# Additions on GpSimd turned into adding transfers in a macaron block with a state-space layer

## The chip, the cores and the metric

The kernel runs on one core of a Trainium2 chip. The metric is the device time of one launch in microseconds (us); the kernel before took 755.14 us, the median of three runs (752.95 to 756.56). A core has five engines with a queue of instructions each: TensorE (PE in the profile), VectorE (DVE), ScalarE (ACT), GpSimd (POOL) and SyncE (SP), which here only begins transfers. Each engine works through its queue in order. An instruction that waits for a semaphore holds up everything behind it on its engine. Transfers (DMAs) are carried by 16 DMA engines that all queues share. A transfer's issue takes time on the engine that begins it, and the transfer lands later.

## The reference

The input is x, 4096 tokens (two sequences of 2048) of 256 numbers, all in 32-bit floating point. Cut to what matters:

```python
def ffn(x):                                  # 8 groups of 512 tokens, each with weights of its own
    h1 = einsum('gmh,goh->gmo', x.reshape(8, 512, 256), W1) + b1[:, None, :]
    return (einsum('gmo,gho->gmh', h1, W2) + b2[:, None, :]).reshape(x.shape)

def ssm(x):
    x_in, z = split(x @ Wi.T + bi)           # 512 channels each
    u  = silu(causal_conv(x_in, conv_w) + conv_b)        # 4 taps for each channel
    dt = softplus(x_in[..., :32] @ Wdt.T + bdt)
    for t in tokens:                         # 512 channels x 16 states
        h = h * exp(dt_t * A) + dt_t * Bm * u_t
        y_t = (h * Cm).sum(-1)
    return (y * silu(z)) @ Wo.T + bo + x * Dv.mean()

x = x + 0.5 * ffn(layernorm(x))
x = x + ssm(layernorm(x))
x = x + 0.5 * ffn(layernorm(x))
```

The network between the two products of `ffn` has no nonlinearity, so the kernel multiplies W1 and W2 once for each group.

## The kernel before, in words

The tokens are taken in four batches of 1024 (`s` from 0 to 3; two batches make a sequence), each in two halves of 512 (`h`). The 512 channels of the state-space layer are taken in four quarters of 128 (`q`). A quarter of a batch is laid out as two tiles of 128 partitions by 512 (`u` = 0 and 1): 64 channels by two halves of the tokens. The first and the last quarter of the whole run are laid out otherwise ("wide": 128 channels, 512 tokens).

The backbone is a row of 256 positions, 64 for each batch and 16 for each quarter. At each position VectorE runs one scan (L698) of 128 by 1024, which takes a decay tile `dec` (ScalarE's exponential, L685, issued three positions ahead) and a drive `pv` in PSUM, which TensorE spreads over the states from the drive `v` (L669). TensorE then reduces the scan's output `g` with the weights `wy` (L707). Everything else is fitted in beside it: the table `PL` gives each step of the preparation a place relative to a position, and the program emits the steps position by position. So the order within each engine's queue is fixed by hand, and no scheduler moves it.

For each quarter the class `Prepare` makes the drive in the 16 positions before it is used. TensorE makes the projections (`inner_pe`), ScalarE writes them into `xi` with the last three columns of the tokens before in front (`inner_act`, `edges`), and `centre` (L531) starts the convolution in the tile `u`, with the tap that needs no shift and the bias. Then come six calls of `tap`: taps 2, 1 and 0 for both tiles, at places t0 to t5 of the table, most of them one or two positions apart. Each call is two GpSimd instructions: a product of shifted `xi` and the channel's weight into the tile `tap` (L536), and the addition of `tap` to `u` (L537). Then `silu` (L604) runs on ScalarE over the whole of `u`. It needs another table of functions, so a table load stands before it; the two Silus of `z` (L601) follow, and a table load back. GpSimd multiplies u by dt into `v` (`drive`, L637), and TensorE spreads that (`spread_v`, L669). The second quarter of the first batch has an order of its own: its taps run three in a row for each tile (places z0 to z2, y0 to y2), and each tile has a Tanh (L582) in place of Silu. The first quarter takes its taps on VectorE.

The tokens themselves lie in tiles `x` of 128 by 4 by 256. Twice a network's result and once the layer's result are added to such a tile. On GpSimd `bias` (L402) adds the network's combined bias row `bc` to all tokens of a tile, `residual` (L454) scales them, `residual_bias` (L458) adds `bo`, and the results of TensorE are added in halves at L421 and L748. VectorE takes the statistics of the layernorm from the tile once the second of its halves is there (`stats_of`, L329); GpSimd then finds the factors (`newton`, L353 to L360) and normalises (L370).

Buffers come from pools with a fixed number of tiles for each name; an instruction that writes a reused tile waits until the last reader of the old contents is done. The tile `tap` has one buffer (pool `p1`), also used for `tz` (L590) and, at the start, for `par_g` (L207). The combined weights `wc` have five (pool `p6`), one for each of the eight groups in turn. Weights, tokens and the copies of `dt` into `rep` (L653) are transfers that SP begins.

Of the kernel before, what the change touches and what calls it, by code (L numbers as in the profile page):

```python
# [28 lines left out]
F32 = mybir.dt.float32  # L29
AF = mybir.ActivationFunctionType  # L30
ALU = mybir.AluOpType
AX = mybir.AxisListType

P = 128
DM = 256
# [9 lines left out]
GT = 4  # L45
NQ = DI // P
# [3 lines left out]
NM = 4  # L50
NH = DM // P
NO = INTER // P
CH = 512
# [21 lines left out]
def macaron_kernel(ctx: ExitStack, tc: tile.TileContext, x, wi_t, wo_t, wdt_t, par, w1, w2_t, b1, b2, bo, out):  # L75
    nc = tc.nc
    V, S, T, GP = nc.vector, nc.scalar, nc.tensor, nc.gpsimd
# [2 lines left out]
    wpool = ctx.enter_context(tc.tile_pool(name="wpool", bufs=2))  # L80
    p1 = ctx.enter_context(tc.tile_pool(name="p1", bufs=1))
    p2 = ctx.enter_context(tc.tile_pool(name="p2", bufs=2))
    p6 = ctx.enter_context(tc.tile_pool(name="p6", bufs=5))
    p3 = ctx.enter_context(tc.tile_pool(name="p3", bufs=3))
    p4 = ctx.enter_context(tc.tile_pool(name="p4", bufs=4))
    p5 = ctx.enter_context(tc.tile_pool(name="p5", bufs=5))
# [6 lines left out]
    def softplus(o, i, bias):  # L93
        return S.activation(o, i, AF.Softplus, bias=bias)
# [38 lines left out]
    bo_all = const.tile([P, 1, DM], F32, name="bo_all")  # L133
# [70 lines left out]
    sel32 = early[:, NPAIR * 2 * NM :][:, :32]  # L204
    sel_rep = const.tile([P, 2, P], F32, name="sel_rep")
    GP.memset(sel_rep, 0.0)
    par_g = p1.tile([P, 3, NQ, 4, NM], F32, tag="tap", name="par_g")  # L207
    a_log, b_g, c_g = (par_g[:, t].rearrange("p q b m -> p (q b m)") for t in range(3))
    neg_a = const.tile([P, NPAIR * 2 * NM], F32, name="neg_a")
    cb_g = early[:, : NPAIR * 2 * NM].rearrange("p (a b) -> p a b", b=1)  # L210
# [41 lines left out]
    wc, bc, held_row, held_wc = {}, {}, {}, {}  # L252
# [132 lines left out]
    class Ffn(Norm):  # L385
# [13 lines left out]
            return self.xt[pair]  # L399

        def bias(self, eng):
            eng.tensor_tensor(self.xs, self.xs, bc[self.g].to_broadcast((P, GT, DM)), ALU.add)  # L402

        def product(self, pair, bias=False):
            pt = self.pt[pair] = bank(f"pf_{self.name}_{pair}")
            for k in range(2):
                o = pt[:, k * DM : (k + 1) * DM]
                for hh in range(NH):
                    T.matmul(o, lhsT=self.xt[pair][:, hh, k * P : (k + 1) * P], rhs=wc[self.g][:, hh, :],  # L409
                             start=(hh == 0), stop=(hh == NH - 1 and not bias))  # L410
                if bias:
                    spread_row(o, held_row[self.g], False)
# [16 lines left out]
    class Second(Norm):  # L429
# [25 lines left out]
                                 ALU.mult, ALU.add)  # L455

        def residual_bias(self):
            GP.tensor_tensor(self.xs, self.xs, bo_all.to_broadcast((P, GT, DM)), ALU.add)  # L458

# [7 lines left out]
    class Prepare:  # L469
# [62 lines left out]
                         scale=self.par(C_CW, NK, u, NK - 1))  # L532

        def tap(self, k, u):
            tap = p1.tile([P, CH], F32, tag="tap", name=f"tap_{self.n}_{k}_{u}")
            GP.tensor_scalar(tap, self.xi[:, u, k : k + CH], self.par(C_CW, NK, u, k), 0.0, ALU.mult, ALU.add)  # L536
            GP.tensor_tensor(self.u[:, u, :], self.u[:, u, :], tap, ALU.add)  # L537

        def tap_dve(self, k, u):
            V.scalar_tensor_tensor(self.u[:, u, :], self.xi[:, u, k : k + CH], self.par(C_CW, NK, u, k),  # L540
# [46 lines left out]
        def gate_z(self, u):  # L587

            z = zs[self.s, self.q]
            self.tz = p1.tile([P, CH], F32, tag="tap", name="tz")  # L590
            S.activation(z[:, u, :], self.pt["z", u], AF.Identity, bias=self.par(C_BI + NQ, 1, u))
            S.activation(self.tz, z[:, u, :], AF.Tanh, scale=0.5)
            self.pt.pop(("z", u))
# [79 lines left out]
    def place_of(t):  # L673
        s, j = divmod(t // NPOS, NPAIR)
        return s, j, *ORDER[t % NPOS]
# [233 lines left out]
    f = second[1]  # L909
# [112 lines left out]
    for t in range(end):  # L1022
        s, j, k, m = place_of(t)
# [76 lines left out]
```

## Time and profile before

| What | Value |
|---|---|
| median of three runs | 755.14 us |
| the profiled execution | 757.39 us |
| its span, first to last instruction | 755.6 us |
| PE, DVE, ACT, POOL busy | 640.1, 639.0, 527.7, 513.7 us |
| POOL on the chain that ended last | 24% of the span |
| granted clock of TensorE, mean | 0.934 |
| DMA: bytes moved, share of the 16 engines on SP's queue | 62.29 MB, 29.4% |

The busy shares are means over stages with different limits. The chain follows the work that ended last back from the end, at each step to what released it. A line of a group gives the source line, the engine, the operation, output and inputs, their shapes and the count; then the busy time in us and the mean of one in ns; then the idle time of the engine just before, and what ended most of it. A line of the waits names who waited for whom, the us in all, the number of times and the longest. A line of the DMA issues gives the line of the tiles, the queue, the count, the size of one and the median us from issue to landing; the issuing time itself is not counted as busy. A line of the timeline has the start and the duration in us.

### The profile page before, as it was taken

The page shows a single profiled execution, that of the slowest core. Times are in us where ns is not written, and L with a number is a line of the kernel's source. Part 1 is how long each engine was busy: PE and PEld are TensorE (multiplying, and loading weights), DVE is VectorE, ACT ScalarE, POOL GpSimd, SP SyncE. Part 2 cuts the span into 40 slices and gives each one's busy share as a digit, 9 for nine tenths or more (in the row PEclk, how much of TensorE's full clock was granted, in tenths as well). Part 3 has the DMA queues.
Part 4 walks back from the last instruction along what each step waited for, and adds up shares of the span by engine and source line. Part 5 has one row for each costly group of instructions (what it writes and reads, how often), then busy time and mean ns, then how long its engine had stood idle before and what let it go on. Part 6 is the DMA issues. An engine that isn't in the chain of part 4 may idle for free.

```text
span 755.6 us, 10374 instructions
## 1 busy us (share of the span) xinstructions
PE 640.1 (85%) x3422; PEld 274.3 (36%) x3422; DVE 639.0 (85%) x553; ACT 527.7 (70%) x658; POOL 513.7 (68%) x821
## 2 busy tenths in 40 slices
PE   9998797994778999897886999897697989777866
PEld 6634241540212554442221654442121434212444
DVE  3487589794899989877899998867898999999994
ACT  3467786682799667756799677656799777868631
POOL 6125658999854878989853797989964778753421
PEclk9999697996899999999799999999799999897979
DMA  8274224152122326334122226313122222322101
GB/s 295 79 218 118 56 85 126 38 152 49 28 57 57 77 63 162 109 103 130 28 57 57 70 64 159 100 56 82 32 57 56 57 56 58 112 56 56 29 1 56
DMA packets 42789, 62.29 MB, mean 82 GB/s; under 512 B 12536, under 2 KB 22128, under 8 KB 42736
## 3 DMA queue, kind: packets, MB, share of 16 engines
q1 hardware_dynamic: 41344, 59.84, 29.4%
q0 software_dynamic: 720, 1.24, 0.6%
q8 instruction: 27, 0.44, 0.3%
q10 hardware_dynamic: 672, 0.56, 0.2%
q14 instruction: 26, 0.21, 0.1%
HBM read 24.08 MB, written 4.19 MB: 37 GB/s over the span
## 4 chain that ended last, share of the span: by engine, by line
PE 36%; POOL 24%; DVE 16%; ACT 10%; issue 8%; DMA 4%; SPq 2%; ACTq 0%; DVEq 0%; POOLq 0%
DVE g L698 13%; POOL u L537 6%; PE po L739 6%; PE pwc L266 6%; PE py L707 6%; ACT dec L685 5%; PE pv L669 4%; POOL tap L536 3%; POOL x L421 3%; PE pf_f L409 3%; PE pxi L495 2%; PE pz L495 2%; POOL x L402 2%; SPq L653 2%; DMA x<-in_x 2%
## 5 line engine op out<-in xcount | busy, mean ns | idle before, releaser
L685 ACT ACTIVATE dec<-rep,neg_a 128x1024 f32<-128x1024 f32 (+1 forms) x280 | 286.0, 1058 | 78.0 <-DVE g L698 69.4
L698 DVE TENSOR_TENSOR_SCAN g<-dec,state,pv 128x1024 f32<-128x1024 f32 (+1 forms) x160 | 309.3, 2002 | 22.3 <-PE py L707 8.3
L698 DVE TENSOR_TENSOR_SCAN g<-dec,pv 128x1024 f32<-128x1024 f32 (+1 forms) x128 | 265.2, 2132 | 23.5 <-PE pv L669 8.6
L707 PE MATMUL py<-g,wy 128*32 128x512 f32 x1024 | 161.5, 652 | 39.7 <-ACT ev_y L714 22.1
L537 POOL TENSOR_TENSOR u<-u,tap 128x512 f32<-128x512 f32 x90 | 114.2, 1269 | 10.9 <-ACT u L531 3.4
L669 PE MATMUL pv<-v,sel_rep 64*128 64x512 f32 (+1 forms) x256 | 77.6, 702 | 27.1 <-POOL v L637 11.7
L700 POOL COPY state<-g 128x1 f32<-128x1 f32 x160 | 27.7, 186 | 81.2 <-DVE g L698 81.2
L718 POOL TENSOR_TENSOR z<-ev_y,z 128x512 f32<-128x512 f32 x31 | 39.5, 1275 | 50.7 <-ACT ev_y L714 50.7
L409 PE MATMUL pf_f<-wc,xnt_f 128*128 128x256 f32 x256 | 66.1, 401 | 7.2 <-ACT xnt_f L380 4.8
L707 PEld LDWEIGHTS py<-g,wy 128*32 128x32 f32 x1024 | 24.0, 112 | 132.3 <-issue 65.3
L536 POOL TENSOR_SCALAR tap<-xi,par_p 128x512 f32<-128x512 f32 x84 | 58.1, 692 | 9.6 <-DMA xi<-xi 6.1
L266 PE MATMUL pwc<-w,w 128*128 128x256 f32 x256 | 61.8, 388 | 0.6 <-DMA w<-in_w_t 0.3
L495 PE MATMUL pz<-xn2t,wi_sb 128*64 128x512 f32 x224 | 60.3, 665 | 1.3 <-ACT ev_f L417 1.3
L409 PEld LDWEIGHTS pf_f<-wc,xnt_f 128*128 128x128 f32 x256 | 47.6, 196 | 30.5 <-ACT xnt_f L380 9.6
L266 PEld LDWEIGHTS pwc<-w,w 128*128 128x128 f32 x256 | 46.6, 190 | 21.1 <-issue 11.1
L739 PE MATMUL po<-wo_sb,z 64*128 64x256 f32 x448 | 52.8, 386 | 1.6 <-POOL z L718 1.6
L495 PE MATMUL pxi<-xn2t,wi_sb 128*64 128x512 f32 x224 | 51.1, 598 | 0.0
L402 POOL TENSOR_TENSOR x<-x,bc 128x1024 f32<-128x1024 f32 x14 | 33.1, 2362 | 24.3 <-ACT xn_f L368 24.2
L739 PEld LDWEIGHTS po<-wo_sb,z 64*128 64x128 f32 x448 | 42.7, 189 | 16.1 <-issue 7.9
L669 PEld LDWEIGHTS pv<-v,sel_rep 64*128 64x128 f32 (+1 forms) x256 | 20.5, 198 | 74.2 <-DVE g L698 31.2
L637 POOL TENSOR_TENSOR v<-u,dt 128x512 f32<-128x512 f32 x28 | 35.0, 1270 | 6.9 <-ACT u L604 6.9
L380 ACT COPY xnt_f<-ptr_f 128x512 f32<-128x512 f32 x31 | 18.0, 588 | 27.2 <-PE ptr_f L377 22.9
(158 smaller groups left out, 759.3 us busy)
## 6 DMA issues: line engine op xcount, KB each, us to landing
rep<-dt SPq DMA_DIRECT2D x496, 64.0 KB, 2.0
w<-in_w SPq DMA_DIRECT2D x16, 512.0 KB, 4.9
w<-in_w_t SPq DMA_DIRECT2D x16, 512.0 KB, 6.5
x<-in_x SPq DMA_DIRECT2D x7, 512.0 KB, 5.6
out<-x SPq DMA_DIRECT2D x6, 512.0 KB, 3.0
wi_sb<-in_wi_t SPq DMA_DIRECT2D x1, 1024.0 KB, 13.7
wo_sb<-in_wo_t SPq DMA_DIRECT2D x2, 512.0 KB, 6.6
out<-x SPq DMA_DIRECT2D x4, 256.0 KB, 2.2
```

Of the source, the lines that this page charges most:

```text
L266: T.matmul(pt, lhsT=a[:, oc, hh * P : (hh + 1) * P], rhs=b[:, oc, :], start=(k == 0 and oc == 0), stop=(k == 1 and oc == NO // 2 - 1),)
L402: eng.tensor_tensor(self.xs, self.xs, bc[self.g].to_broadcast((P, GT, DM)), ALU.add)
L409: T.matmul(o, lhsT=self.xt[pair][:, hh, k * P : (k + 1) * P], rhs=wc[self.g][:, hh, :], start=(hh == 0), stop=(hh == NH - 1 and not bias))
L495: T.matmul(pt[h * HC : (h + 1) * HC, :], lhsT=wi_sb[:, hh, k : k + HC], rhs=xn2t[self.s, h][:, hh, :], start=(hh == 0), stop=(hh == NH - 1))
L536: GP.tensor_scalar(tap, self.xi[:, u, k : k + CH], self.par(C_CW, NK, u, k), 0.0, ALU.mult, ALU.add)
L537: GP.tensor_tensor(self.u[:, u, :], self.u[:, u, :], tap, ALU.add)
L669: T.matmul(t[:, c * CH : (c + 1) * CH], lhsT=sel_rep[r, c if is_wide(s, j) else a, :], rhs=v_sb[s, j // NJ2][r, j % NJ2, :], start=True, s ...
L685: S.activation(decs[t][:, c * w : (c + 1) * w], part, AF.Exp, scale=neg_a[:, i : i + 1])
L698: V.tensor_tensor_scan(g[:, r], dec[:, r], v[:, r], 0.0 if first else state[:, i : i + 1], ALU.mult, ALU.add)
L707: T.matmul(pys[s, j][rows(is_wide(s, j), a, c), :], lhsT=wy[:, column(s, j, a, c, m), :], rhs=gs[a, m][:, c * CH : (c + 1) * CH], start=(m ...
L718: GP.tensor_tensor(z, held_ev.pop((s, j)), z, ALU.mult)
L739: T.matmul(held_po[s, pair][h][:, k * DM : (k + 1) * DM], lhsT=lhsT, rhs=rhs, start=((q, i) == parts[0]), stop=((q, i) == parts[-1]))
```

## The change

Three additions on GpSimd become transfers that GpSimd begins and that add to their destination: the tap's addition to `u`, and the addition of `bc` and of `bo` to a tile of tokens. A bias row is read four times by the transfer, once for each group of 256 numbers of a partition. `tap` moves to the pool with two buffers, and with it the other two tiles of that name. The pool of `wc` has four buffers, not five. The program places the waits: a reader of `u` or of `x` waits for the landing, the next addition to the same tile waits for the landing of the one before, and the product that reuses a tap buffer waits for the landing of the transfer that reads it.

```diff
-    p6 = ctx.enter_context(tc.tile_pool(name="p6", bufs=5))
+    p6 = ctx.enter_context(tc.tile_pool(name="p6", bufs=4))
...
-    par_g = p1.tile([P, 3, NQ, 4, NM], F32, tag="tap", name="par_g")
+    par_g = p2.tile([P, 3, NQ, 4, NM], F32, tag="tap", name="par_g")
...
         def bias(self, eng):
-            eng.tensor_tensor(self.xs, self.xs, bc[self.g].to_broadcast((P, GT, DM)), ALU.add)
+            GP.dma_start(self.xs, bc[self.g].to_broadcast((P, GT, DM)), accum_op=ALU.add)
...
         def residual_bias(self):
-            GP.tensor_tensor(self.xs, self.xs, bo_all.to_broadcast((P, GT, DM)), ALU.add)
+            GP.dma_start(self.xs, bo_all.to_broadcast((P, GT, DM)), accum_op=ALU.add)
...
         def tap(self, k, u):
-            tap = p1.tile([P, CH], F32, tag="tap", name=f"tap_{self.n}_{k}_{u}")
+            tap = p2.tile([P, CH], F32, tag="tap", name=f"tap_{self.n}_{k}_{u}")
             GP.tensor_scalar(tap, self.xi[:, u, k : k + CH], self.par(C_CW, NK, u, k), 0.0, ALU.mult, ALU.add)
-            GP.tensor_tensor(self.u[:, u, :], self.u[:, u, :], tap, ALU.add)
+            GP.dma_start(self.u[:, u, :], tap, accum_op=ALU.add)
...
         def gate_z(self, u):
-            self.tz = p1.tile([P, CH], F32, tag="tap", name="tz")
+            self.tz = p2.tile([P, CH], F32, tag="tap", name="tz")
```

## The prediction

> **What bounds the kernel now.** I read the page first (busy shares, then the chain that ended last), then the waits, then the timeline round the places where the change acts, then the DMA issues.
>
> ```profile
> PE 36%; POOL 24%; DVE 16%; ACT 10%; issue 8%; DMA 4%; SPq 2%; ACTq 0%; DVEq 0%; POOLq 0%
> ...
> L537 POOL TENSOR_TENSOR u<-u,tap 128x512 f32<-128x512 f32 x90 | 114.2, 1269 | 10.9 <-ACT u L531 3.4
> L402 POOL TENSOR_TENSOR x<-x,bc 128x1024 f32<-128x1024 f32 x14 | 33.1, 2362 | 24.3 <-ACT xn_f L368 24.2
> ```
>
> No engine is full (PE and DVE 85%, ACT 70%, POOL 68%). The chain changes hands: POOL carries it in a few stretches, PE and DVE in others. The first line gives POOL 24% of 755.6 us, about 181 us; in the chain in order of time most of that lies at 148 to 196, 291 to 320, 343 to 367, 465 to 491, 516 to 541 and 633 to 653 us. What POOL's lateness costs there is in the waits:
>
> ```profile
> DVE st_l L329 <- POOL x L421: 28.9, 12, 5.6
> DVE g L698 <- PE pv L669: 13.2, 6, 2.7
> ACT u L604 <- POOL u L537: 8.1, 3, 2.8
> ```
>
> (us in all, times, longest.) VectorE loses 28.9 us to late row sums on POOL and 13.2 us at the start of a new quarter, where TensorE spreads the new drive `v`. So about 42 us is the most that a lighter POOL could give back. Outside those stretches the end of the taps meets ScalarE. The timeline of the fourth change of quarter (ScalarE, GpSimd, VectorE; start, duration in us):
>
> ```profile
> 229.54 1.28 ACT L604 ACT_TABLE_LOAD   x1
> 230.96 1.06 ACT L604 ACTIVATE u<-u 128x1024 f32<-128x1024 f32 x1
> 231.92 1.25 ACT L601 ACTIVATE z<-pz,par_p 128x512 f32<-128x512 f32 x2
> 233.19 1.28 ACT L573 ACT_TABLE_LOAD   x1
> 234.48 3.23 ACT L685 ACTIVATE dec<-rep,neg_a 128x1024 f32<-128x1024 f32 x3
> ...
> 229.66 1.26 POOL L537 TENSOR_TENSOR u<-u,tap 128x512 f32<-128x512 f32 x1
> ...
> 236.12 2.32 DVE L698 TENSOR_TENSOR_SCAN g<-dec,state,pv 128x1024 f32<-128x1024 f32 x1
> ```
>
> The last tap addition runs under ScalarE's table load (1.28 us) and ends as the load ends; Silu follows, two more Silus, a table load back, and then the decay that the new quarter's first scan needs. That decay ends at 235.63 (234.48 plus one 1.15), and its scan starts at 236.12: 0.49 us of slack. I worked this slack out for every later change of quarter: 0.49, 0.61 and 0.49 us at 231, 403 and 576 us (ScalarE is busy 19 us of 20 there), 1.2 to 1.5 at 193, 365, 538, 651 and 686, 1.9 to 3.0 at the rest.
>
> **The change part by part.** It removes 90 additions of 1.27 us and 22 row additions of 2.36 us from POOL: 114.2 + 33.1 + 8 × 2.37 = 166 us. It adds 112 DMA issues on POOL, and what is new in latency. Nothing moves on PE, ACT, DVE or SP; the built programs differ only in these rows and in their waits.
>
> *Issue on POOL.* The trace has plain DMAs issued by POOL, none that adds:
>
> ```profile
> L653 POOL DMA_DIRECT2D rep<-dt x8: 496/496/607, 66.9 to 70.4; - x8
> ...
> L159 POOL DMA_DIRECT2D par_w<-in_par x1: 607/607/607, 8.8 to 8.8; - x1
> ...
> rep<-dt POOLq DMA_DIRECT2D x8, 64.0 KB, 2.7
> ...
> rep<-dt SPq DMA_DIRECT2D x496, 64.0 KB, 2.0
> out<-x SPq DMA_DIRECT2D x6, 512.0 KB, 3.0
> out<-x SPq DMA_DIRECT2D x4, 256.0 KB, 2.2
> ```
>
> 32 rows cost 496 ns, 128 rows 607, or 1.2 ns a row. A tap has 128 rows: 0.61 us. A row addition has 512 pieces of 1 KB (its source repeats): 0.61 to 1.05; I take 1.05, by the slope. So POOL saves 0.66 us a tap and 1.31 a row addition, 59 + 29 = 88 us of its time.
>
> *Landing.* From issue to landing 64 KB by POOL takes 2.7 us, 0.7 over SP; the `out` rows give 0.8 us per further 256 KB. A plain 256 KB is then 2.7 + 0.6 = 3.3 us. An adding transfer also reads its destination: another 256 KB, 0.8, so L = 4.1 for a tap; for a row addition R = 2.7 + 1.4 + 1.6 = 5.7. Lower ends: the extra read is free (3.3, 4.1); upper ends: it costs twice as much (4.9, 7.3). I take the middle because the data are read twice. A rule of the Trainium skill speaks for less: "DMA: Bandwidth & Descriptors", section "Anatomy of one DMA — SWDGE (gpsimd) path", fits about 2.0 us plus bytes over 436 GB/s, so L = 2.6 and R = 3.2 as an estimate. But it would give 2.15 for the 64 KB row that took 2.7 here; I keep the row and leave the rule for the first rival.
>
> *The last tap.* In all 14 later quarters the table load of L604 gets the wait for the last tap's landing (before, only the Silu itself waited). So the load no longer hides: Silu starts at the issue + L + 1.28 + about 0.03 instead of the issue + 1.3, that is 4.1 us later, and everything on ScalarE behind it with it. Less the slack: 3.6 us at 231, 3.5 at 403, 3.6 at 576 = 10.7. At 439 and 686 us the tap was earlier than needed: 0.7 each. At 651 POOL's savings ahead of it pay most: 0.9. At 269 and 613 nothing: the taps end 4 to 5 us early. Of these places the chain itself runs through 231 and 576.
>
> *The second quarter's taps* (72 to 98 us) are three in a row on one half-tile, each of which must wait for the one before it to land. First half: issued at 73.26, ready at 73.26 + 3 × 4.1 = 85.6; the Tanh that needs it started at 81.28: 4.3 us on ScalarE, which has decays just in time behind it. Second half: 90.68 + 12.3 = 103.0 against 97.53, 5.5 late; the decay behind has 1.98 of slack, and VectorE sits 2.8 us idle at 113.4 anyway, so I take 2.5. Behind the waiting issues POOL holds state copies and a `b_pad` copy; VectorE needs a copy five scans later, which these 4 us don't reach.
>
> *The second tap buffer* lets the next product run while one transfer is under way; the third product waits for the first's landing. Taps lie 4.3 us (n to n+2) at the tightest, product first 0.7: under 1 us of POOL each, beside idle POOL time in the quarters where it occurs.
>
> *POOL's stretches, gain.* 148 to 196: by 175 us three row additions and two taps are off the queue (5.25 us), but L421 must now wait for the row addition of the same tile, issued at 170.82 − 3.28 and landed 5.7 later, 173.2: gain 2.2 there, 4.2 at the next sum, and at the last tap 4.1 + 1.3 of gain against 4.1 of later Silu; 2.5 us remain at the scan. 291 to 320: five taps and a row addition, 4.6, less 0.8 for a landing, against 4.1; `v` then starts 3.4 earlier, because it stood behind L402 in the queue: 2.7. The same at 465 to 491, where VectorE waits longer (3.5): 3.0. 343 to 367 and 516 to 541: L421 waits for the row addition issued 4.4 us ahead of it, so the gain is 0.6 to 1.3 and the later Silu takes it: −0.3 each. Sum 7.6.
>
> *The tail.* The last row addition starts at 746.80; landed at 752.5 it holds the final two sums (0.69 each), which started at 749.75 and 751.48: 1.7 us.
>
> *The rest.* One `wc` buffer less: the write of group 4 waits for a product of group 0 that the next ScalarE row waited for already: 0. Added traffic is 90 × 256 KB + 22 × 512 KB = 34 MB beside 62, on engines busy 30%; the `rep` transfers that a decay waits for (8.2 us now) lose an estimated 1.0.
>
> A rule that speaks against the change: "SBUF — State Buffer", section "SBUF: two separate sides", says that a VectorE operation in a two-port mode keeps GpSimd from writing descriptors until it ends. POOL's additions here take 1259/1268/1289 ns (least, median, most) under a VectorE that scans all the time; with the rule in force they would scatter. By the trace this costs nothing; by the rule each of 112 issues could wait half a scan, 1.1 us, and POOL would lose its whole gain (+8 us).
>
> *Sum:* 10.7 + 0.7 + 0.7 + 0.9 + 4.3 + 2.5 + 1.7 + 1.0 = 22.5 lost, 7.6 gained: +14.9. The profiled execution took 757.4 us (span 755.6, 1.8 round it), so 772.3 there; the median of the runs lies 2.3 lower, which gives 770, slower by 2%.
>
> **Rivals.** *Transfers land fast* (faster). With L = 2.6, R = 3.2 the losses are 6.2 at the three tight places, 0.3 in the tail, nothing in the second quarter; POOL's stretches give 5.5, 4, 4, 3 and 3 = 19.5. 755 − 13 = 742. For it: the skill's fit, and 42 us of VectorE waits to win back. Against it: the 2.7 us row. The losses grow by 6 to 9 us for each us of L and the gains shrink; the sign turns at L of about 3.3. *The adding is slow* (L = 4.9, R = 7.3): 31 lost, 1.5 gained: 785. For it: nothing in the trace shows the rate of an adding transfer; against: the engines are idle 70% of the time. *Hidden anyway*: gains and losses cancel, 755, if L lies at 3.3 to 3.4.
>
> **How the numbers follow.** Chances: the main forecast (L 3.5 to 4.6) 0.46, slow adding 0.22, fast landing 0.25, cancelling 0.07. A run can tell about 0.5% from no change, 3.8 us. Faster 0.25, same 0.07, slower 0.68. The range for 8 in 10 takes in the fast case down to 742 and slow adding up to 797; the main case alone spans 761 to 779.
>
> **What would show it.** In the profile of after: POOL's busy time near 350 us, about 0.6 us an issue on L537; landing of `u<-tap` near 4.1 us; ACT's wait at L604 for a DMA in nearly all 14 quarters, 50 us in all; `st_l` behind L421 still waiting, less than 29 us. The prediction is wrong if landing is under 3.3 us, or if issues take well over 1 us and POOL becomes the bound.

## The result, and the profile after

The changed kernel takes 837.3 us (median of four runs, 825.8 to 839.2); beside it the kernel before took 755.9. One of the four, 839.2, is a slow run; the ratio of the fast ones is 1.103, with an interval of 1.091 to 1.115. Slower was forecast; the size was not: +82 us over the 755.1 on record came where +15 was worked out, and 837 lies far outside the range of 742 to 797. The profiled execution took 836.4 us, its span is 834.6, 79.0 more than before.

Three lines of the page: the chain that ended last, by engine and by line, and GpSimd's group of tap transfers.

```profile
PE 23%; DMA 19%; POOL 14%; ACT 12%; DVE 7%; issue 6%; SPq 4%; ACTq 0%; DVEq 0%; POOLq 0%
DMA u<-tap 11%; DVE g L698 5%; PE pxi L495 5%; DMA x<-bc 5%; PE py L707 4%; ACT dec L685 4%; PE pwc L266 4%; PE pv L669 4%; SPq L653 4%; POOL tap L536 3%; PE po L739 2%; ACT L604 2%; DMA rep<-dt 2%; DMA x<-in_x 2%; POOL u L537 2%
...
L537 POOL DMA_DIRECT2D u<-tap x90 | 80.4, 893 | 35.4 <-POOL tap L536 25.9
```

GpSimd's share of the chain fell from 24% to 14%, as a lighter GpSimd should do, but transfers rose from 4% to 19%, and 16 of these 19 are landings of what was added: of taps (11) and of `bc` rows (5).

The waits (us in all, times, longest):

```profile
ACT L604 <- DMA u<-tap: 62.3, 14, 9.9
...
DVE st_l L329 <- POOL x L421: 41.4, 9, 10.0
DVE g L698 <- PE pv L669: 37.5, 7, 9.6
DVE g L698 <- ACT dec L685: 31.8, 13, 6.0
...
POOL u L537 <- POOL tap L536: 25.9, 85, 0.9
POOL x L421 <- DMA x<-bc: 22.1, 3, 9.1
```

The two waits of VectorE that the change was to shorten have grown, from 28.9 to 41.4 us and from 13.2 to 37.5. All 14 later changes of quarter now have ScalarE waiting for the last tap, and scans wait 31.8 us for a decay, 6.9 before. GpSimd's additions of the networks' results (L421) wait 22.1 us for three rows.

The fourth change of quarter, shown before at 229 us, on the timeline (start, duration, in brackets the idle time before):

```profile
255.18 0.89 POOL L537 DMA_DIRECT2D u<-tap  x1 [0.30 <-POOL tap L536]
...
259.24 1.28 ACT L604 ACT_TABLE_LOAD   x1 [4.43 <-DMA u<-tap]
260.54 1.06 ACT L604 ACTIVATE u<-u 128x1024 f32<-128x1024 f32 x1
261.50 1.25 ACT L601 ACTIVATE z<-pz,par_p 128x512 f32<-128x512 f32 x2
...
265.30 4.59 DVE L698 TENSOR_TENSOR_SCAN g<-dec,state,pv 128x1024 f32<-128x1024 f32 x2 [4.10 <-ACT dec L685]
```

Issue at 255.18, landed 4.00 later, and only then the table load, which before lay under the addition. The scan stands still for 4.10 us.

What GpSimd pays for one tap is seen where it issues two in a row:

```profile
239.10 0.68 POOL L536 TENSOR_SCALAR tap<-xi,par_p 128x512 f32<-128x512 f32 x1
240.08 0.89 POOL L537 DMA_DIRECT2D u<-tap  x1 [0.30 <-POOL tap L536]
240.70 1.01 POOL L536 TENSOR_SCALAR tap<-xi,par_p 128x512 f32<-128x512 f32 x1
242.00 0.88 POOL L537 DMA_DIRECT2D u<-tap  x1 [0.30 <-POOL tap L536]
242.58 0.51 POOL L700 COPY state<-g 128x1 f32<-128x1 f32 x1
```

The issue waits 0.30 us for the product; the next instruction begins 0.62 after the issue, while the issue's record still runs (0.89), and takes 0.32 longer than elsewhere: 1.01 for a product that takes 0.69, 0.51 for a copy that takes 0.18. Product to product that is 1.60 + 0.32 = 1.92 us; before, from the product at 218.78 to the next instruction at 220.76, it was 1.98. A tap transfer frees GpSimd of 0.06 us, not of 0.66.

The landings (issue to landing, median us for each kind of tiles):

```profile
rep<-dt SPq DMA_DIRECT2D x496, 64.0 KB, 2.8
u<-tap POOLq DMA_DIRECT2D x90, 256.0 KB, 4.2
...
x<-bc POOLq DMA_DIRECT2D x14, 512.0 KB, 6.6
x<-bo_all POOLq DMA_DIRECT2D x8, 512.0 KB, 6.2
```

The median of a tap is the L = 4.1 of the sum; those of the rows lie 0.5 and 0.9 over its R = 5.7. The spread is what the sum left out. The lines of the two transfers asked for one by one:

```profile
L537 POOL DMA_DIRECT2D u<-tap x90: 857/887/970, 73.9 to 759.9; - x90
...
DMA to landing us min/median/max: 3.3/4.2/11.7
```

and for the `bc` rows:

```profile
L402 POOL DMA_DIRECT2D x<-bc x14: 1280/1599/1646, 148.2 to 824.2; - x14
...
DMA to landing us min/median/max: 5.4/6.6/12.5
```

A tap can take 11.7 us and a row 12.5. But the 14 taps right ahead of a Silu all landed in 3.3 to 4.4 us; the late ones are others, and so are their waiters. The three rows that L421 waits for took 11.75, 12.53 and 8.67 us. The first of them, and the two queues while it was on its way (packets, MB, share of the 16 engines' time; q0 is GpSimd's, q1 is SP's):

```profile
185.71 1.61 POOL L402 DMA_DIRECT2D x<-bc  x1
...
197.60 1.26 POOL L421 TENSOR_TENSOR x<-ev_f,x 128x512 f32<-128x512 f32 x1 [8.03 <-DMA x<-bc]
...
q0 software_dynamic: 1187, 1.39, 75.4%
q1 hardware_dynamic: 549, 1.40, 37.9%
```

The packets' time adds up to 113% of what 16 engines have, two thirds of it GpSimd's own. The "engines busy 30%" of the sum was a mean over the span.

**Where the 79 us lie.** For each place I took the start of the first scan behind it in both traces, after minus before, and then the difference to the place ahead. "Taps" and "rows" are the same figure for the kernels with only the taps or only the rows as transfers, which are told below. A gain is negative.

| Place (us, before) | put in the sum | measured | taps alone | rows alone |
|---|---|---|---|---|
| second quarter, first half (82) | 4.3 | 4.2 | 3.8 | 0.1 |
| second quarter, second half (to 108) | 2.5 | 4.6 | 4.8 | 0 |
| change of quarter at 143 | 0 | 8.1 | 8.1 | -0.1 |
| 148 to 196 | -2.5 | 6.9 | 3.0 | 3.4 |
| changes at 231, 403, 576 | 10.7 | 13.2 | 13.1 | 0.6 |
| 291 to 320 | -2.7 | 7.3 | 5.1 | -0.3 |
| 343 to 367 | 0.3 | 8.7 | 3.2 | 6.3 |
| 465 to 491 | -3.0 | 7.9 | 5.9 | -1.2 |
| 516 to 541 | 0.3 | 6.7 | 3.3 | 1.5 |
| changes at 439, 651, 686 | 2.3 | 8.2 | 4.5 | 0 |
| tail | 1.7 | 2.2 | 1.5 | 1.8 |

What is left (1.0 us) lies scattered; the 1.0 us put down for `rep` has no place of its own. The five stretches in which GpSimd is full give 37.5 us of loss where 7.6 of gain stood in the sum. That is 45 of the 64 us by which the sum was short; the change at 143 us is 8 more. The loss in the stretches has two parts: 20.5 us appear at the changes of quarter that close them, and 16.9 ahead of these: 13.4 in the three stretches where VectorE waits for the sums of L421, 3.5 in the other two (291 and 465). With the taps alone the parts are 21.2 and -0.8, with the rows alone -2.4 and 12.1. So the taps hurt at the changes, and the rows ahead of them.

### The profile page after: what moved, and what is told of

Its sections match the earlier page's. It is cut to its first block, busy times and chain, and to the rows that moved or that the text cites. A ratio compares the mean times of both kernels' runs of the same rounds, so it can differ in the third digit from the quotient of the medians.

```text
span 834.6 us, 10446 instructions
## 1 busy us (share of the span) xinstructions
PE 656.3 (79%) x3422; PEld 278.8 (33%) x3422; DVE 639.1 (77%) x553; ACT 526.4 (63%) x658; POOL 463.3 (56%) x821
## 3 DMA queue, kind: packets, MB, share of 16 engines
q0 software_dynamic: 25296, 36.37, 26.9%
## 4 chain that ended last, share of the span: by engine, by line
PE 23%; DMA 19%; POOL 14%; ACT 12%; DVE 7%; issue 6%; SPq 4%; ACTq 0%; DVEq 0%; POOLq 0%
DMA u<-tap 11%; DVE g L698 5%; PE pxi L495 5%; DMA x<-bc 5%; PE py L707 4%; ACT dec L685 4%; PE pwc L266 4%; PE pv L669 4%; SPq L653 4%; POOL tap L536 3%; PE po L739 2%; ACT L604 2%; DMA rep<-dt 2%; DMA x<-in_x 2%; POOL u L537 2%
## 5 line engine op out<-in xcount | busy, mean ns | idle before, releaser
L707 PE MATMUL py<-g,wy 128*32 128x512 f32 x1024 | 165.2, 675 | 53.7 <-ACT ev_y L714 39.1
L669 PE MATMUL pv<-v,sel_rep 64*128 64x512 f32 (+1 forms) x256 | 80.1, 723 | 39.7 <-POOL v L637 30.0
L537 POOL DMA_DIRECT2D u<-tap x90 | 80.4, 893 | 35.4 <-POOL tap L536 25.9
L536 POOL TENSOR_SCALAR tap<-xi,par_p 128x512 f32<-128x512 f32 x84 | 72.8, 867 | 35.2 <-DMA u<-tap 24.1
L700 POOL COPY state<-g 128x1 f32<-128x1 f32 x160 | 43.9, 319 | 73.7 <-DVE g L698 73.5
L266 PE MATMUL pwc<-w,w 128*128 128x256 f32 x256 | 66.0, 408 | 19.6 <-ACT z L601 19.3
L495 PE MATMUL pz<-xn2t,wi_sb 128*64 128x512 f32 x224 | 63.4, 693 | 6.8 <-ACT ev_f L417 3.5
L718 POOL TENSOR_TENSOR z<-ev_y,z 128x512 f32<-128x512 f32 x31 | 42.2, 1362 | 47.7 <-ACT ev_y L714 47.5
L266 PEld LDWEIGHTS pwc<-w,w 128*128 128x128 f32 x256 | 49.1, 200 | 41.0 <-ACT z L601 22.0
L604 ACT ACT_TABLE_LOAD x14 | 18.0, 1283 | 62.3 <-DMA u<-tap 62.3
L421 POOL TENSOR_TENSOR x<-ev_f,x 128x512 f32<-128x512 f32 x24 | 35.2, 1480 | 33.9 <-DMA x<-bc 22.1
```

The source lines that it names most:

```text
L266: T.matmul(pt, lhsT=a[:, oc, hh * P : (hh + 1) * P], rhs=b[:, oc, :], start=(k == 0 and oc == 0), stop=(k == 1 and oc == NO // 2 - 1),)
L495: T.matmul(pt[h * HC : (h + 1) * HC, :], lhsT=wi_sb[:, hh, k : k + HC], rhs=xn2t[self.s, h][:, hh, :], start=(hh == 0), stop=(hh == NH - 1))
L537: GP.dma_start(self.u[:, u, :], tap, accum_op=ALU.add)
L669: T.matmul(t[:, c * CH : (c + 1) * CH], lhsT=sel_rep[r, c if is_wide(s, j) else a, :], rhs=v_sb[s, j // NJ2][r, j % NJ2, :], start=True, s ...
L700: GP.tensor_copy(state[:, i : i + 1], g[:, (c + 1) * w - 1 : (c + 1) * w])
L707: T.matmul(pys[s, j][rows(is_wide(s, j), a, c), :], lhsT=wy[:, column(s, j, a, c, m), :], rhs=gs[a, m][:, c * CH : (c + 1) * CH], start=(m ...
```

## The experiments

The theory after the result: what costs is a landing that somebody waits for with nothing to cover it, with whatever is queued behind that wait. The rivals: the transfers cost by their traffic or by GpSimd's work for them, wherever they lie. In the diffs `-` is the changed kernel where nothing else is said.

**1. The rows alone** (the changed kernel, its buffers too, with line 537 of the one before).

```
-            GP.dma_start(self.u[:, u, :], tap, accum_op=ALU.add)
+            GP.tensor_tensor(self.u[:, u, :], self.u[:, u, :], tap, ALU.add)
```

> The 22 row additions as adding transfers, the taps added by GpSimd as before (buffers as in the changed kernel). Theory A (each landing that something waits for costs where it is waited for, the rows at the sum behind them, L421): the rows still land 8 us and more late beside the weight loads, L421 waits, 760 to 772 us. Theory B (it is the 90 taps in the same queue that make the rows late): without the taps the rows land in about 5.5 to 6.5 us, L421 waits under 3 us in all, GpSimd is lighter by some 20 us: 748 to 757 us.

Measured: 767.9 us, ratio 1.015 (1.010 to 1.019). A row costs GpSimd a little less (1.33 us of issue for 2.36 of addition), and yet this loses. The first loss is at 180 us; on the timeline of this kernel:

```profile
168.34 1.29 POOL L402 DMA_DIRECT2D x<-bc  x1
...
179.82 1.26 POOL L421 TENSOR_TENSOR x<-ev_f,x 128x512 f32<-128x512 f32 x1 [7.84 <-DMA x<-bc]
```

The row was issued where the sum put it (167.5), but landed after 11.35 us, not 5.7: while it was on its way SP's queue moved 1.75 MB and GpSimd's 0.87. GpSimd stood 7.84 us ahead of L421. The same at 348 us (11.55).

**2. The taps alone** (the changed kernel with lines 402 and 458 of the one before).

> The 90 taps as adding transfers, the rows added by GpSimd as before (buffers as in the changed kernel). Theory A: the last taps' landings, with the table load behind them, and the second quarter's rows of three hold most of the 82 us; 800 to 820 us, and ScalarE still waits about 55 to 60 us at L604. Theory B (taps and rows hurt each other in one queue): clearly under half of the 82 us, 775 to 795 us.

818.4 us, ratio 1.082 (1.078 to 1.085). The taps cost 63 of the 82 us; 63 and 13 make 76, so some 6 come only with both (8.5 in the profiled spans), though the interval of the result is as wide as that.

**3. The buffers alone** (`tap` with two, `wc` with four, all additions on GpSimd).

> No transfer that adds: the changed kernel's buffers alone (two for the tap, four for the combined weights). Both theories: no change, 752 to 758 us. If the lost weight buffer or the second tap buffer did part of it, over 760 us or under 750 us.

756.5 us, ratio 1.001 (0.999 to 1.003): nothing, as the sum had it.

**4. The last tap of each tile on GpSimd.**

```
-            GP.dma_start(self.u[:, u, :], tap, accum_op=ALU.add)
+            if k == 0:
+                GP.tensor_tensor(self.u[:, u, :], self.u[:, u, :], tap, ALU.add)
+            else:
+                GP.dma_start(self.u[:, u, :], tap, accum_op=ALU.add)
```

> The changed kernel, but tap 0 of each half-tile, the last of three, is added by GpSimd itself; taps 2 and 1 and the rows stay transfers. Theory A: ScalarE's 62 us of waits at L604 go to under 12 us, and with them some 40 to 50 us: 780 to 800 us. Theory B (the queue's load is the cause, not who waits last): a third of the tap traffic goes, 805 to 825 us.

782.9 us, ratio 1.035 (1.032 to 1.038). A third of the tap transfers carries 54 us: those with a Silu or a Tanh next.

**5. The same without the rows.** Only the four earlier tap additions of a quarter are transfers.

> The changed kernel with the third tap of each half (k = 0) and all row additions back on GpSimd: only the four earlier tap additions of a quarter are transfers, and no landing stands directly ahead of a Silu. Theory A (parts add up; the run with rows as well stood at 782.9, rows alone cost 12.7): 768 to 773, so 13 to 17 us over the kernel before for issues, buffer waits and the second quarter. Theory B (the taps' cost is the last landing alone): 754 to 760.

760.7 us, ratio 1.007 (1.005 to 1.009). The parts do not add up to 768; the other theory put for this run, that the last landing is all that the taps cost, fits but for 0.7 us. 60 transfers with no Silu right behind them cost 5 us over the kernel before. In the profile it is 6.0, and 4.8 of these lie at one place, the change at 143 us, where a landing is waited for after all:

```profile
133.01 0.68 POOL L536 TENSOR_SCALAR tap<-xi,par_p 128x512 f32<-128x512 f32 x1 [2.68 <-DMA u<-tap]
```

The tap issued at 125.11 landed after 7.80 us, and this product needs its buffer. The run also shows that rows and taps do not simply add: beside these 60 taps the rows cost 22 us, alone 13.

**6. The table load ahead of the wait.**

```
         def silu(self):
+            S.preload_act_table_set("silu_and_others")
             S.activation(self.u, self.u, AF.Silu)
```

> The changed kernel, with the Silu table asked for by an instruction of its own ahead of the Silu, so that the table load (1.28 us, 14 of them, which in the changed kernel start only when the last tap has landed) no longer stands behind the landing. Theory A (the landing gates, and the table load is served in line with it): 1.3 us off at each of the 11 or so changes of quarter at which the scans stand still for the Silu, so 14 to 16 us less: 819 to 825 us. Theory B (at these places the scan waits for something else, such as the matmuls ahead of the v product on TensorE): under 5 us less, 832 to 838.

818.5 us, 19 below the changed kernel: the load that inherits the wait is worth 16 us in the profiled spans and 19 in the medians. But at the changes at 143, 321 and 494 us it gave little: 7.7, 6.4 and 4.6 us were lost there, where the changed kernel loses 8.1, 6.1 and 5.5. On the timeline of this kernel at the first of the three (the Silu of u, the Silus of z, and TensorE):

```profile
151.86 1.06 ACT L605 ACTIVATE u<-u 128x1024 f32<-128x1024 f32 x1 [7.53 <-DMA u<-tap]
152.82 1.25 ACT L601 ACTIVATE z<-pz,par_p 128x512 f32<-128x512 f32 x2
153.00 2.49 POOL L638 TENSOR_TENSOR v<-u,dt 128x512 f32<-128x512 f32 x2 [2.46 <-ACT u L605]
...
153.54 3.78 PE L266 MATMUL pwc<-w,w 128*128 128x256 f32 x8 [7.44 <-ACT z L601]
...
157.12 2.54 PE L409 MATMUL pf_f<-wc,xnt_f 128*128 128x256 f32 x8
...
159.58 1.13 PE L670 MATMUL pv<-v,sel_rep 64*128 64x512 f32 x4
```

`v` is there at 155.49, but 16 matmuls of the feed-forward network stand ahead of `pv` in TensorE's queue, and these wait for z's Silus, which stand behind u's on ScalarE. `pv` starts 4.1 us late. The 16 also run slower than in the kernel before:

```profile
138.22 1.99 PE L266 MATMUL pwc<-w,w 128*128 128x256 f32 x8
140.05 1.89 PE L409 MATMUL pf_f<-wc,xnt_f 128*128 128x256 f32 x8
141.87 1.13 PE L669 MATMUL pv<-v,sel_rep 64*128 64x512 f32 x4
```

From the first of them to `pv` it was 3.65 us and is 6.04, 2.4 of the 4.1. The clock granted to TensorE, 1.00 there before, is 0.50 from 153.5 to 157.2 us, behind 7.44 us without work. In the changed kernel the same piece takes 5.3 us at each of the three changes, at a clock of 0.50 to 0.60, so each of these waits costs some 1.7 us more than it lasts.

**7. z's Silus ahead of u's**, which takes the 16 matmuls, and the table load with them, out of the wait.

```
         def silu(self):
+            self.start_z()
+            for u in range(NJ2):
+                self.silu_z(u)
             S.activation(self.u, self.u, AF.Silu)
-            self.silu_zs()
+            self.exp_table()
```

> The changed kernel with z's two Silus and the table load ahead of u's Silu, so that the TensorE matmuls that wait for z's bank do not stand behind the landing. Theory A (at three changes of quarter the v product is late because 16 matmuls queued ahead of it start only after z's Silus): 19 us as with the table ahead, about 1.2 us more at some ten changes, and 3 to 4 us at those three: 793 to 803. Theory B (TensorE's order does not matter, only the table load): 804 to 818.

808.4 us. By the total this is the rival's range. By place the theory's mechanism is there, and larger than put: at the three changes 3.4, 0.4 and -0.1 us are lost in place of 7.7, 6.4 and 4.6 with the table load alone, 15 us in all, which is the whole difference of the two spans (803.2 against 818.4; the medians lie 10 apart, for the profiled execution is the shortest of the one kernel's runs and the longest of the other's). What did not come is the 1.2 us at the ten other changes, and why not is open. The same place as above, with the 16 at a granted clock of 1.00:

```profile
144.11 1.99 PE L266 MATMUL pwc<-w,w 128*128 128x256 f32 x8
...
145.94 1.89 PE L409 MATMUL pf_f<-wc,xnt_f 128*128 128x256 f32 x8
...
150.94 1.06 ACT L607 ACTIVATE u<-u 128x1024 f32<-128x1024 f32 x1 [7.02 <-DMA u<-tap]
...
153.39 2.08 PE L672 MATMUL pv<-v,sel_rep 64*128 64x512 f32 x4 [5.56 <-POOL v L640]
```

**8. The sixth tap earlier in the plan** (`t5` of the table `PL`: from 11.1, 10.3, 10.2, 11.4 to 9.0, 8.8, 9.5, 9.0).

> The changed kernel with the sixth tap of each quarter issued earlier in the plan (place 8.8 to 9.5 of the quarter's 16 steps instead of 10.2 to 11.4; the Silu is at 12), so that its landing lies beside other work. Theory A (what costs is that the last landing has no cover): the Silu's waits for a landing (62 us in the changed kernel) fall below 25, and the time to 795 to 815. Theory B (the taps are late because GpSimd waits for the two tap buffers and for the landings before, so an earlier place is not an earlier issue): 825 to 838.

810.8 us, 27 below the changed kernel; the Silu's waits for a landing fall from 62.3 to 28.0 us. The changes at 231, 403 and 576 us now lose 0, 0.7 and 0.5 us, where each cost over 4. In the five stretches 27.8 of the 37.5 us stay lost. There GpSimd is behind its plan: the last tap goes out at most one scan of the quarter's 16 earlier, in the quarters without feed-forward work mostly one or two.

**9. Both (8 and 6).**

> The same, with the Silu table asked for ahead of the Silu as well. Theory A: where the landing has cover the table load has it too, so only 3 to 8 us below the run beside it (790 to 808). Theory B: another 16 us below it, as in the changed kernel, because the landing still gates.

804.0 us, 7 below the run before it: where more landings have cover, the load is worth 7 us and not 19.

**10. The second quarter's taps on GpSimd.**

> The changed kernel with the six taps of the second quarter (70 to 110 us) added on GpSimd as before, all others as transfers. Theory A (its two waits for the landing, 3.8 and 8.1 us, are paid once and never won back): 8 to 11 us less, 826 to 829. Theory B (the later quarters would have been late anyway, and the time saved is lost at the next change): under 4 us less, 833 to 838.

827.6 us, 10 less (7.2 in the profiled spans): most of what this place loses, 8.8 us by 108 us in the table, is never won back.

**11. Taps that copy instead of adding.** This leaves out the sum of the taps: each overwrites `u`.

```
-            GP.dma_start(self.u[:, u, :], tap, accum_op=ALU.add)
+            GP.dma_start(self.u[:, u, :], tap)
```

> The changed kernel, with the 90 tap transfers copying instead of adding (what is left out: the sum of the taps, u is overwritten by each). Theory A (the adding in the transfer is what makes the landing late): the landing falls from 4.2 to about 3 us, and the time by some 15 to 25 us, to 812 to 822. Theory B (landing is that of GpSimd's queue and of the traffic beside it, whether it adds or not): landing 3.8 to 4.2 us, time 828 to 838.

808.4 us, 29 less. The issues and landings of this kernel:

```profile
L537 POOL DMA_DIRECT2D u<-tap x90: 567/584/671, 73.7 to 733.9; - x90
...
DMA to landing us min/median/max: 2.3/3.2/11.2
```

Adding costs 1.0 us of landing and 0.30 of issue, and the stretching of the next instruction is gone too (a product right behind an issue takes 0.70 us, not 0.98). The queue's packets take 18.9% of the 16 engines' span, adding 26.9%, for the same 36.37 MB. With copied taps (the rows still add) 53 us of loss remain.

**12. Without the later weight loads**, in the changed kernel and in the one before. What is left out: groups 3 and on use the weights of group 2.

```
     def load_w_part(g, k, i):
+        w_sb[g, k] = w_sb[2, k]
+        return
         view = (w1, w2_t)[i][g].rearrange("(p oc) h -> p oc h", p=P)
```

> The changed kernel without the 20 weight loads (512 KB each) of feed-forward groups 3 and on, which use the weights of group 2 (what is left out). Theory A (the late landings are those beside weight loads): row landings fall from 6.6 to about 5.5 us median and none is over 8; the waits of the additions for a row (22 us) nearly vanish, and the time falls to 815 to 826. Theory B (GpSimd's own transfers stand one behind the other, or wait for the rep transfers): landings as before, time 830 to 838.

> The kernel before without the same 20 weight loads, as the base for the run beside it. Both theories: nobody waits for them there, 750 to 757 us. The difference between the two is 60 to 74 us by Theory A, 77 to 86 by Theory B.

822.2 and 755.8 us: the difference is 66, not 82. So some 15 us of the loss come with the weight loads. By place, about 10 of them lie in the five stretches ahead of the changes, where the rows are waited for (16.9 to 6.3 us). But the median landing of a `bc` row fell only from 6.6 to 6.4 us, the longest from 12.5 to 8.7; two of the three waits of L421 for a row stayed (22.1 to 9.9 us). The row issued at 183.55 still took 8.34 us, and in that time GpSimd's own queue moved 1.3 MB, packets enough to fill the 16 engines (105%). The theory is right on the late ones and not the whole of it: GpSimd's transfers delay each other too.

**13. Only what has cover.** First the eight `bo` rows alone, then these with the first tap of each tile (k = 2), the second quarter left out.

> The kernel before with only the eight additions of the output bias (2.37 us each on GpSimd) as adding transfers; nobody waits for these within 10 us. Theory A (what costs is a landing that somebody waits for): no loss, 750 to 757, with up to 4 us gained at the three stretches where GpSimd is full. Theory B (the traffic or the issue itself costs): 758 to 762.

755.0 us, ratio 0.997 (0.995 to 0.999) in 14 runs: perhaps 2 us better, under what a measurement of this kernel can tell by the bound set above.

> Only what nobody should wait for goes as a transfer: the eight output-bias rows, and the first tap of each half (k = 2) outside the second quarter. Theory A (cost comes with a landing that somebody waits for; a tap transfer saves GpSimd 1.27 - 0.89 us and loses about 0.3 us of wait for the product): 750 to 758, no measurable gain over the eight rows alone. Theory B (each tap transfer costs by the traffic it makes): 760 to 768.

763.4 us, ratio 1.010 (1.006 to 1.013). The rival fits by the time, but the run above with 60 tap transfers lost less (760.7) than this one with 28, so traffic alone does not explain it. In the profile (759.4, the shortest of its six) 4.0 us go at the change at 143 us: a product at 130.81 waits 2.44 us for the buffer of a tap that landed after 7.68. That may not be all of it, for the run with the eight rows alone lost 4.2 us there too, ahead of its first adding transfer, and won 3.3 back by 183 us. What the rest is I can't say.

**14. All covers together**: 8, 7, the second quarter's taps and the `bc` rows on GpSimd.

> All covers together: last tap issued earlier in the plan, z's two Silus (with the table load) ahead of u's, second quarter's taps and the feed-forward bias rows on GpSimd; the other tap additions and the output-bias rows as transfers. Theory A: from 804 (last tap earlier, table ahead) less 13 for the rows, 10 for the second quarter and about 5 for z: 772 to 782, still slower than before because in the stretches with feed-forward work the taps cannot be issued early enough. Theory B (all of the cost was cover): 750 to 760.

776.1 us, ratio 1.027 (1.023 to 1.031). So 61 us of the 82 go with a better order and with 20 of the 112 transfers taken back (the order alone, in run 9, took 33), and 21 stay. No version here beats the kernel before by more than a measurement can tell.

## Why the prediction was wrong, point by point

**What held.** The table load gets the wait, and the last taps at 231, 403 and 576 us cost 13.2 us for 10.7. The second quarter's first half cost 4.2 for 4.3, the tail 2.2 for 1.7, the buffers nothing. The landings' medians, 4.2 and 6.2 to 6.6 us, are those of the middle values, so the rival of a fast landing falls (estimates of 2.6 and 3.2 by the fit of the Trainium skill, "DMA: Bandwidth & Descriptors", section "Anatomy of one DMA — SWDGE (gpsimd) path"; no tap landed in under 3.3), and that of a slow adding too (4.9 and 7.3). The checkpoint of ScalarE's waits (14 quarters, 50 us) stood at 14 and 62.3.

**The step that failed** is "POOL's stretches, gain": -7.6 put, +37.5 measured. Three of its terms were wrong; the change at 143 us, put at nothing, fell with the third.

- *What GpSimd saves.* 0.66 us a tap was put, 0.06 is had: the issue takes 0.89 us and not 0.61 (copying it takes 0.58, so a plain DMA's row was a fair one for a copy and a bad one for adding), it waits 0.30 for the product, and it stretches the instruction behind it. A row saves 1.0 for 1.31: at 182.66 the next instruction starts 0.80 us on and is stretched by 0.52. So GpSimd is relieved of about 28 us in all (90 × 0.06 + 22 × 1.04), not 88, and the stretches had no lead to win. The two checkpoints for this, 0.6 us an issue on L537 and 350 us of busy time on GpSimd, stand at 0.89 and 463. The page counts the records of GpSimd's issues as busy, contrary to what I wrote ahead of the prediction; without them GpSimd was busy 502.9 us before and 369.9 after, 133 less for 166 of additions. But the price of the issue is not the main thing: with copied taps, whose issue costs 0.58 and stretches nothing, the stretches still lose 26.8 us.
- *What lands there.* The sum took one L and one R for all places, from transfers with nothing beside them. In these stretches the feed-forward network's weights are loaded and the rows go out close to the taps, on engines that are full and not 30% busy, and the three rows that matter took 8.7 to 12.5 us. L421 waits for them (8.03 us at 197.6, 9.11 at 393.7), where the sum put gains of 0.6 to 2.2. This is most of the 16.9 us ahead of the changes, which are 12.1 with the rows alone and 6.3 without the weight loads.
- *What stands behind a late Silu.* The sum followed ScalarE and the decay. This is the 20.5 us at the changes, and there the landings were the usual ones. At 143, 321 and 494 us the end is set by TensorE: z's Silus hold matmuls that stand ahead of `pv`, and these then run at about half the clock. "`v` then starts 3.4 earlier", the gain put at 291 to 320, became 6 us of loss at the change that closes it. Moving z ahead brought 15 us back at these three places. For 143 us the sum had nothing at all, on the strength of 1.9 to 3.0 us of slack for "the rest" of the changes; the slack was real for the decay only.

**Smaller misses.** The second tap buffer was to cost under 1 us of GpSimd for a wait; its products wait 26.8 us in all, 24 times, at most 3.2. The second half of the second quarter took 4.6 us, not 2.5: I set VectorE's idle 2.8 us at 113.4 against it, and it did not absorb the delay. At 651 us GpSimd's savings were to pay, and 6.1 us were lost; at the change itself it is 5.3, and 1.8 with the table ahead. `rep` lands after 2.8 us and not 2.0, and decays wait 19.0 us for it, 8.2 before, more than the 1.0 put; how much of that is on the path no run tells.

**The rule on descriptors.** That a two-port VectorE operation keeps GpSimd from writing them (the Trainium skill, "SBUF — State Buffer", section "SBUF: two separate sides") did not show: 90 adding issues take 857 to 970 ns and 90 copying ones 567 to 671, with VectorE busy 77% of the span in the first kernel, mostly with scans. The scatter of half a scan (1.1 us) is not there; the long issue is the adding's. Whether a scan is an operation of that kind no trace tells, so this is no test of the rule itself.

**Why the range failed.** Every case in it had the landing as one number and followed a late Silu along ScalarE alone. The slow rival raised L for all places to 4.9 and got 31 us of losses. The case that came was not among them: taps that land as put ahead of the Silus but hold TensorE's order, and rows that take 8.7 to 12.5 us where they are waited for.

## What to carry to other kernels

A transfer in place of an engine's operation is paid twice, in the issue on the engine that begins it and in the landing, so first look who reads the result next, who needs the source's buffer, and what else is queued behind these on every engine, TensorE's order included; only a result that nobody reads for longer than a landing beside full traffic (here 12 us, not 4) is free to go. Price the landing from the traffic at the place and not from a median, and the issue from a row of the same kind: one that adds, not one that copies. Where such a wait can't be avoided, put ahead of it in the queue what doesn't need it: the table load, the other Silus.

## What the runs showed of the hardware

An adding transfer begun by GpSimd costs more than a copy of the same 256 KB in all respects: 0.89 us of issue for 0.58, 4.2 us to land for 3.2, and half as much packet time again (26.9% of 834.6 us is 225, 18.9% of 805.5 is 152, each in time of all 16 engines and with the rows). Its packets are more as well, 25296 for 19536 on the queue.

I had not expected that GpSimd's next instruction starts before the issue's record ends and runs slower beside it: a copy of one column took 0.51 us for 0.18 behind an adding issue, and 0.20 behind a copying one. So the duration of an issue alone tells neither what it costs nor what it hides.

Nor had I counted on TensorE's clock. Behind waits of 4.65 to 9.81 us its next matmuls ran at a granted clock of 0.50 to 0.60, at the three changes of quarter above. Over the whole run the mean fell from 0.934 to 0.901, and TensorE's busy time for the same 3422 matmuls rose from 640.1 to 656.3 us; how much of these 16 us is on the path outside the three places no run tells.
